# A message-passing kernel on one core: every place in its written-out instruction order chosen anew

## The chip, the cores and the metric

One NeuronCore of a Trainium2 chip (trn2). The metric is device time in microseconds (us) of one launch; lower is better. The five engines that matter here are TensorE (PE; its weight loads are listed as PEld), VectorE (DVE), ScalarE (ACT), GpSimd (POOL) and SyncE (SP, which here only issues DMAs).

## The reference

128 graphs of 64 nodes with 128 features, an adjacency of about one pair in eight. For every pair a three-layer network makes a message from both nodes' features, the messages are masked by the adjacency and summed over the neighbours, and a second network of the same form updates each node.

```python
def _mlp(x, w0, b0, g0, be0, w1, b1, g1, be1, w2, b2):
    h = jax.nn.relu(x @ w0 + b0)
    h = _layernorm(h, g0, be0)
    h = jax.nn.relu(h @ w1 + b1)
    h = _layernorm(h, g1, be1)
    return h @ w2 + b2
...
pair_feats = jnp.concatenate([f_i, f_j], axis=-1)
messages = _mlp(pair_feats, msg_w0, ...)
messages = messages * coupling_matrix[..., None]
agg = jnp.sum(messages, axis=2)
updated = part_feats + _mlp(jnp.concatenate([part_feats, agg], axis=-1), upd_w0, ...)
```

## The kernel before

The kernel computes messages only for the pairs that the adjacency holds. Two graphs make a pair of graphs p (64 of them), four such pairs make a block b (16), and the edges of a graph are packed into 640 places. The places are cut into 160 chunks n of 4 x 128 edges; five chunks make a group q (32 groups), over which the small vectors of the normalization are computed. Ten chunks belong to one block, so the work repeats with a period of ten chunks.

For each block, VectorE numbers the edges along each row of the adjacency (`rank`, line 731, a scan) and forms a flag for weights other than 0 and 1 (`odd_weights`, 811 and 812); a small matmul counts them, and GpSimd turns the counts into places (`place`, 749 to 767, and `place_out`, 776). For each pair of graphs ScalarE and VectorE form a 128 x 640 table of which node owns which place (`distance` 876, then `make_tp` 882). GpSimd widens it (`node_rows`, 891), TensorE and VectorE find the neighbour's number (`marks` 908, `compare` 916), and SP's DMAs lay both halves into the selection matrix s (`stack`, 898). TensorE then gathers the first layer's rows for each chunk (`gather`, 933), ScalarE applies the bias and the relu (`relu0`, 938), TensorE transposes (`turn_h`, 943, into the one bank hT), and VectorE takes the statistics (`stats0`, 629, out st<-hT). ScalarE or GpSimd prepares the second layer's shift (`seed` 980, `seed_all` 973), TensorE multiplies (`layer1`, 986), ScalarE or VectorE applies the relu (`relu1`, 997 or 613), and VectorE takes the statistics again (`stats1`, 629, out st<-y). When the last of a group's ten `stats1` is there, GpSimd adds up the variance (`var1_step`, 646 and 647, tile m_v), ScalarE takes the root (`root1_of`, 653, tile m_sq), VectorE inverts it (`inverse_of`, 658), GpSimd makes the weights (`weights`, 1029), and TensorE sums the messages of a whole block (`reduce_block`, 1044: 96 matmuls on end, once in a period). The node update follows with `bias0` (1082, 1083) and `residual` (1087) on GpSimd, three layers (1111) and `finish` (1159) with the store (1162).

There is no scheduler at run time. Each engine runs its instructions in the order in which they were written, and waits at the first one whose inputs or buffers are not ready. That order is written by a plan. Every step is entered with a chunk number n and a tag; its key is 144 n plus a number from the table `WHEN`, read by the step's name and tag, and in the steady part (chunks 14 to 137) by n modulo 10, otherwise by 100 plus the step's own index. The steps are then sorted by this key and issued.

```python
def at(n, tag, fn, *args):
    ...
    t = WHEN.get(f"{fn.__name__}{tag}", {}).get(n % 10 if 14 <= n < 138 else 100 + v, 0)
    plan.append((SCALE * n + t, len(plan), fn, args))
...
for _, _, fn, args in sorted(plan, key=lambda v: v[:2]):
    fn(*args)
```

The buffers that bear on the order: one bank each for hT, for hps (the gather's result) and for mk (`marks`), two for z, two i tables and two j tables, three u tiles, four selection matrices s.

Of the kernel before, what the change touches and what calls it, by code (L numbers as in the profile page):

```python
# [25 lines left out]
    "<lambda>.3": {100: 398},  # L26
    "<lambda>.4": {100: 795},
    "<lambda>.6": {100: 4632},
    "<lambda>.7": {100: 284},
    "ahead.0": {100: 233},  # L30
    "ahead.1": {100: 132},
    "ahead.10": {100: 11},
    "ahead.11": {100: -1},
    "ahead.2": {100: 50},
    "ahead.5": {100: 113},
    "ahead.8": {100: 157},
    "ahead.9": {100: 215},
    "bias0": {3: -1471, 112: -1906, 113: -1642, 114: -17},
    "bias0_0": {115: 1153},
    "bias0_2": {115: 525},  # L40
    "bounds": {100: -15375},
# [8 lines left out]
    "count": {8: -190, 101: 140, 102: 122, 115: -186},  # L50
    "count.0": {100: 47},
    "count_out": {9: -228, 101: -2, 102: 190, 115: -239},
    "count_out.0": {100: 63},
    "degrees": {9: -358, 101: -137, 102: 105, 115: -608},
    "degrees.0": {100: -699},
    "distance": {0: -539, 3: 150, 5: -495, 8: -349, 103: 84, 104: 283, 105: -140, 106: 202,
        107: -511, 108: 189, 158: -852, 159: -528, 160: -749, 161: -525, 162: -737, 163: -1005},
    "distance.0": {100: 181},
    "distance.1": {101: 189},
    "distance.2": {102: 311},  # L60
    "empties.0": {100: 111},
    "empties.1": {100: 152},
    "empties.10": {100: 200},
    "empties.11": {100: 169},
    "empties.2": {100: -14},
    "empties.3": {100: 100},
    "empties.4": {100: 111},
    "empties.5": {100: 55},
    "empties.6": {100: -50},
    "empties.7": {100: -92},  # L70
    "empties.8": {100: -22},
    "empties.9": {100: 128},
    "finish": {8: 220, 110: 217, 111: 771, 112: 335, 113: -14, 114: 4865},
    "finish_0": {115: 6154},
    "finish_2": {115: 6519},
    "flag_in": {100: 118},
    "flag_max": {100: 160},
    "flag_out": {100: 377},
    "flag_sum": {100: 514},
    "flag_turn": {100: 45},  # L80
# [26 lines left out]
    "inverse_of": {0: -228, 5: 130, 125: -359, 126: -111, 127: 59, 128: 506, 129: 147, 130: 64,  # L107
# [44 lines left out]
    "layer_out.uh": {7: -98, 112: 370, 113: 251, 114: 103},  # L152
    "layer_out.uy": {2: 270, 111: -27, 112: 407, 113: 290, 114: 1108},
# [1505 lines left out]
```

## Time and profile before

| what | value |
|---|---|
| three runs | 501.89, 500.96, 501.84 us; median 501.84 |
| the profiled execution's own time | 501.05 us |
| its span, first to last instruction | 499.3 us |
| granted TensorE clock, mean | 0.997 |
| busy in the span: PE, DVE, ACT, POOL | 97%, 94%, 80%, 70% |
| span less busy time, PE | 13.2 us, of it 3.2 us between 50 us and 475 us |
| span less busy time, DVE | 31.3 us |

The span is the time between the first and the last instruction of the program; 1.75 us of the execution's own time lie around it. An engine's share is the time in which at least one of its instructions was running, so an instruction that runs slowly because something holds it up counts as busy. Matmuls overlap, and their ends are modelled: a stall of TensorE is seen in full only as the distance between two starts, and up to about 0.16 us of it is hidden in the busy time (a 128 x 128 matmul is drawn 275 ns long, and the next starts 112 ns after it).

### The profile page before, as it was taken

The page shows a single profiled execution, that of the slowest core. Times are in us where ns is not written, and L with a number is a line of the kernel's source. Part 1 is how long each engine was busy: PE and PEld are TensorE (multiplying, and loading weights), DVE is VectorE, ACT ScalarE, POOL GpSimd, SP SyncE. Part 2 cuts the span into 40 slices and gives each one's busy share as a digit, 9 for nine tenths or more (in the row PEclk, how much of TensorE's full clock was granted, in tenths as well). Part 3 has the DMA queues.
Part 4 walks back from the last instruction along what each step waited for, and adds up shares of the span by engine and source line. Part 5 has one row for each costly group of instructions (what it writes and reads, how often), then busy time and mean ns, then how long its engine had stood idle before and what let it go on. Part 6 is the DMA issues. An engine that isn't in the chain of part 4 may idle for free.

```text
span 499.3 us, 15949 instructions
## 1 busy us (share of the span) xinstructions
PE 486.1 (97%) x5947; PEld 460.6 (92%) x5947; DVE 468.0 (94%) x1225; ACT 397.1 (80%) x907; POOL 349.1 (70%) x563
## 2 busy tenths in 40 slices
PE   7999999999999999999999999999999999999996
PEld 4889999999999999989999998999989999999995
DVE  7999999999999999999999999999999998989985
ACT  6989978878787887868878786887868779867845
POOL 3275776967949776696877859776696859555771
PEclk9999999999999999999999999999999999999998
DMA  4766838376564756646486673666655458626231
GB/s 122 152 140 152 183 100 162 82 165 153 125 139 98 139 142 150 148 113 142 97 167 142 125 152 90 136 137 147 142 122 135 95 120 163 145 68 154 59 41 47
DMA packets 91474, 63.55 MB, mean 127 GB/s; under 512 B 57473, under 2 KB 75522, under 8 KB 91394
## 3 DMA queue, kind: packets, MB, share of 16 engines
q1 hardware_dynamic: 91106, 62.36, 57.7%
q8 instruction: 49, 0.80, 0.7%
q14 instruction: 31, 0.25, 0.2%
q10 hardware_dynamic: 288, 0.13, 0.1%
HBM read 7.15 MB, written 4.19 MB: 23 GB/s over the span
## 4 chain that ended last, share of the span: by engine, by line


## 5 line engine op out<-in xcount | busy, mean ns | idle before, releaser
L986 PE MATMUL z<-w1c,h 128*128 128x128 f32 x1280 | 190.1, 275 | 0.0
L986 PEld LDWEIGHTS z<-w1c,h 128*128 128x128 f32 x1280 | 172.4, 192 | 4.1 <-DVE uy_st L629 0.2
L938 ACT ACTIVATE h<-hps,b0c 128x512 f32<-128x512 f32 x160 | 108.9, 681 | 35.0 <-PE hps L933 34.5
L629 DVE BATCH_NORM_STATS2 st<-hT 128x6 f32<-128x256 f32 x320 | 122.4, 415 | 6.7 <-PE hT L943 5.1
L629 DVE BATCH_NORM_STATS2 st<-y 128x6 f32<-128x256 f32 x320 | 126.9, 418 | 1.6 <-ACT y L997 1.5
L980 ACT ACTIVATE z<-b1b,m_sd 128x128 f32<-128x128 f32 x320 | 117.3, 368 | 9.4 <-DVE y L613 3.7
L943 PE MATMUL hT<-ident,h 128*128 128x128 f32 x640 | 113.0, 276 | 1.9 <-DVE st L629 1.8
L933 PE MATMUL hps<-s,abl 128*128 128x512 f32 (+3 forms) x256 | 96.9, 381 | 2.6 <-ACT h L938 2.2
L933 PE MATMUL hps<-s,abh 128*128 128x512 f32 (+3 forms) x256 | 89.9, 358 | 0.0
L973 POOL TENSOR_TENSOR u<-b1b,m_sd 128x512 f32<-128x512 f32 x80 | 84.3, 1057 | 7.7 <-ACT m_sd L637 7.7
L943 PEld LDWEIGHTS hT<-ident,h 128*128 128x128 f32 x640 | 75.9, 141 | 6.3 <-issue 3.1
L1029 POOL TENSOR_TENSOR w<-oh,m_q 128x192 f32<-128x192 f16 x126 | 62.0, 513 | 8.8 <-DVE m_q L658 2.5
L916 DVE TENSOR_TENSOR j<-mk,cmpt 128x320 fp32r<-128x320 f32 x124 | 59.2, 477 | 6.3 <-PE mk L908 3.6
L891 POOL CAST i<-tp 128x640 fp32r<-128x640 f16 x58 | 41.7, 719 | 32.1 <-DMA s<-i 30.1
L997 ACT ACTIVATE y<-z 128x512 f32<-128x512 f32 x80 | 47.4, 595 | 17.7 <-PE z L986 17.3
L613 DVE CUSTOM_DVE_ANT_0 y<-z,u 128x512 f32<-128x512 f32 x80 | 54.0, 675 | 3.6 <-PE z L986 3.3
L933 PEld LDWEIGHTS hps<-s,abl 128*128 128x128 f32 x256 | 48.8, 191 | 7.7 <-ACT h L938 3.7
L876 ACT ACTIVATE d<-slot,mid 128x640 f16<-128x640 f16 x64 | 52.1, 818 | 1.7 <-POOL mid L765 1.0
L933 PEld LDWEIGHTS hps<-s,abh 128*128 128x128 f32 x256 | 49.1, 192 | 0.2
L647 POOL TENSOR_TENSOR m_v<-m_v,st 128x20 f32<-128x20 f32 x31 | 7.2, 232 | 58.5 <-DVE st L629 57.3
L1044 PE MATMUL ys<-y,w 128*32 128x128 f32 x1488 | 44.1, 274 | 0.0
L1044 PEld LDWEIGHTS ys<-y,w 128*32 128x32 f32 x1488 | 39.6, 110 | 2.5 <-issue 2.1
(193 smaller groups left out, 890.7 us busy)
## 6 DMA issues: line engine op xcount, KB each, us to landing
s<-i SPq DMA_DIRECT2D x124, 160.0 KB, 3.1
s<-j SPq DMA_DIRECT2D x124, 160.0 KB, 2.9
xn<-in_x_dram SPq DMA_DIRECT2D x15, 256.0 KB, 3.9
out_dram<-uo SPq DMA_DIRECT2D x15, 256.0 KB, 2.5
an<-in_adj_dram SPq DMA_DIRECT2D x16, 128.0 KB, 3.4
oh<-tp SPq DMA_TRANSPOSE x64, 3.2
xn<-in_x_dram SPq DMA_DIRECT2D x2, 128.0 KB, 3.0
out_dram<-uo SPq DMA_DIRECT2D x2, 128.0 KB, 2.0
```

What stands on the lines that cost most here:

```text
L613: nc.vector._custom_dve(TENSOR_ADD_SAT, out=o, in0=ps, in1=sb, s0=BIG, s1=0.0)
L629: nc.vector.bn_stats(st, src.rearrange("p t c -> p c t"))
L876: nc.scalar.activation(D[p], slot, AF.Abs, bias=blocks[b]["mid"][:, q:q + 1], scale=-1.0)
L916: nc.vector.tensor_tensor(JR[p][:, c], MK.pop((p, k))[:, 0:HC], cmpt[:, c], op=ALU.is_equal)
L933: nc.tensor.matmul(HP[n][:, c:c + w], lhsT=blocks[g // (2 * PB)]["ab", g // 4 % 2][k][:, g % 4, :], rhs=S[g // 2][:, g % 2, e:e + w], star ...
L938: nc.scalar.activation(H[n], HP.pop(n), AF.Relu, bias=b0c)
L943: nc.tensor.transpose(HT[n][:, t, :], H[n][:, t * P:(t + 1) * P], ident)
L973: nc.gpsimd.tensor_tensor(U[n], bc(W["b1b"], CH), SR[q][:, k:k + CH].unsqueeze(2).to_broadcast([P, CH, C]), op=ALU.mult)
L980: nc.scalar.activation(z_of(n)[:, t, :], W["b1b"], AF.Copy, scale=SR[q][:, k:k + 1])
L986: nc.tensor.matmul(ps[:, t, :], lhsT=H[n][:, t * P:(t + 1) * P], rhs=W["w1c"], start=by_vector(n) and t == 0, stop=True, skip_group_check= ...
L1029: (nc.vector if p == NP - 2 else nc.gpsimd).tensor_tensor(WT[p][:, g], oh, qs, op=ALU.mult)
L1044: nc.tensor.matmul(YS[b][g * N + m * HN:g * N + (m + 1) * HN, k, :], lhsT=w[:, g, m, u, :], rhs=y, start=(u == 0), stop=(u == TH - 1), til ...
```

## The change

Only the numbers in `WHEN` are replaced: all of its entries are chosen anew, and the table is two lines shorter, so line numbers of the kernel after are smaller by 2 (`stats1` at 629 is at 627). No instruction is added, removed or changed in size; the buffers, the choice of engine for each step and the chunk at which a step is entered stay. By the words that go with the change, VectorE's `rank`, `make_tp` and `odd_weights` are to be kept clear of GpSimd's operations, and later landings of DMAs are allowed for.

```diff
-    "rank": {6: -208, 101: 117, 102: -33},
+    "rank": {6: -172, 101: 62, 102: -12},
...
-    "residual": {9: 658, 111: 1661, 112: 1065, 113: 1049, 114: 3450},
+    "residual": {9: -202, 111: 2069, 112: 835, 113: 1274, 114: 2138},
```

What the numbers do is seen in the order of the engines. **VectorE in a period of the steady part, around `rank`,** from the two `stats0` rows ahead of it to the last `stats1` of the group. In before the group's statistics tile is st_4540, st_4724 is the next group's, st_4583 holds `stats0`, tp is written by `make_tp`, j by `compare`; the scan of `rank` is printed here as SCALAR_TENSOR_TENSOR.

```order
L629 BN_STATS st_4583<-hT 128x6 x2
L731 SCALAR_TENSOR_TENSOR rk<-first,an 128x256
L629 BN_STATS st_4540<-y 128x6
L882 TENSOR_SCALAR tp<-d,deg 128x640
L629 BN_STATS st_4540<-y 128x6
L1359 MEMSET ones_row 1x128
L629 BN_STATS st_4540<-y 128x6
L629 BN_STATS st_4724<-y 128x6
L629 BN_STATS st_4583<-hT 128x6
L629 BN_STATS st_4540<-y 128x6
L629 BN_STATS uy_st<-uy 128x6
L629 BN_STATS st_4583<-hT 128x6
```

The same place after, where st_4527 is this group's tile, st_4575 holds `stats0` and st_4725 is the next group's:

```order
L627 BN_STATS uy_st<-uy 128x6
L627 BN_STATS st_4575<-hT 128x6 x2
L627 BN_STATS st_4527<-y 128x6
L914 TENSOR_TENSOR j_4750<-mk,cmpt 128x320
L627 BN_STATS st_4527<-y 128x6
L729 SCALAR_TENSOR_TENSOR rk<-first,an 128x256
L627 BN_STATS st_4575<-hT 128x6 x2
L914 TENSOR_TENSOR j_4750<-mk,cmpt 128x320
L880 TENSOR_SCALAR tp<-d,deg 128x640
L627 BN_STATS st_4527<-y 128x6
```

Five statistics that followed `rank` now stand ahead of it: three of the group's, one of the next group's, one of the node update's. The two `stats0` of the next chunk follow it at once. Of the two `compare` of a pair, the first stood ahead of the five statistics that preceded `rank` and now has one of them behind it; the second stood behind the group's last `stats1` and now precedes it, as `make_tp` and `rank` did already. (The MEMSET fills a row of constants and bears on nothing here.)

**GpSimd at the same place,** from `node_rows` (i) to the variance of the group (m_v). In before:

```order
L891 CAST i_4594<-tp 128x640
L973 TENSOR_TENSOR u<-b1b,m_sd 128x512
L1082 TENSOR_TENSOR m_4604<-c2u,deg 128x512
L1083 TENSOR_TENSOR m_4604<-m_4604,ub0r 128x512
L1087 TENSOR_TENSOR xo<-xn,cu2b 128x512
L973 TENSOR_TENSOR u<-b1b,m_sd 128x512
L776 TENSOR_TENSOR posall<-pos,an 64x4x64 x2
L646 TENSOR_SCALAR m_v<-st_4019 128x20
L647 TENSOR_TENSOR m_v<-m_v,st_4540 128x20
```

and after:

```order
L971 TENSOR_TENSOR u<-b1b,m_sd 128x512 x2
L1027 TENSOR_TENSOR w<-oh,m_q 128x192
L774 TENSOR_TENSOR posall<-pos,an 64x4x64 x2
L889 CAST i_4727<-tp 128x640
L1080 TENSOR_TENSOR m_4732<-c2u,deg 128x512
L1081 TENSOR_TENSOR m_4732<-m_4732,ub0r 128x512
L971 TENSOR_TENSOR u<-b1b,m_sd 128x512
L644 TENSOR_SCALAR m_v<-st_4011 128x20
L645 TENSOR_TENSOR m_v<-m_v,st_4527 128x20
```

Between `node_rows` and the variance stand three operations where seven stood: `residual` (xo) has gone, the two `seed_all` (u) and the two `place_out` (posall) are ahead of `node_rows`, and one later `seed_all` has come in.

**GpSimd half a period later,** ahead of the second variance of the period, from the low half of the first layer's rows (abl). In before:

```order
L864 TENSOR_TENSOR abl<-ab,abh 128x512
L973 TENSOR_TENSOR u<-b1b,m_sd 128x512
L646 TENSOR_SCALAR m_v<-st_4322 128x20
L647 TENSOR_TENSOR m_v<-m_v,st_4724 128x20
L891 CAST i_5025<-tp 128x640
```

and after:

```order
L862 TENSOR_TENSOR abl<-ab,abh 128x512
L971 TENSOR_TENSOR u<-b1b,m_sd 128x512
L1085 TENSOR_TENSOR xo<-xn,cu2b 128x512
L1027 TENSOR_TENSOR w<-oh,m_q 128x192 x2
L644 TENSOR_SCALAR m_v<-st_4331 128x20
L645 TENSOR_TENSOR m_v<-m_v,st_4725 128x20
```

Here `residual` and two `weights` have come in between.

TensorE's order changes in small ways throughout: in the steady part, pairs of transposes of the node update trade places with half a `layer1`, or a `gather` with a transpose. On SP the load of the next adjacency is issued a few DMAs earlier, and two transposing DMAs of `node_marks` stand together ahead of the two halves of a j table (`stack`) that one of them parted. At the end, all four matmuls of the second-last block's third layer stand ahead of the last chunk's `layer1`, where two stood in the middle of it and two behind, and on VectorE that block's `finish` stands ahead of five of the last `stats1` instead of two. At the start, ScalarE's copy of the turned features comes ahead of the first two `distance`, and the third `distance` ahead of the first `node_rows`-like copy (line 1347).

More of the change, by code (lines that the diff above doesn't have):

```diff
@@ L25 @@
 WHEN = {
[L26 to L41, printed above, removed]
[8 rows of a table removed]
@@ L50 @@
[L50 to L75, printed above, removed]
@@ L370 @@
-    "weights.1.1": {2: -269, 7: -112, 151: -490, 153: 294, 155: 117, 157: 234, 159: 279, 161: 259,
-        163: 359},
+    "<lambda>.3": {100: -2537},
+    "<lambda>.4": {100: 3097},
+    "<lambda>.6": {100: 5123},
+    "<lambda>.7": {100: -79},
+    "ahead.0": {100: 256},
+    "ahead.1": {100: 84},
+    "ahead.10": {100: 0},
+    "ahead.11": {100: 76},
+    "ahead.2": {100: 60},
+    "ahead.5": {100: -84},
+    "ahead.8": {100: 146},
+    "ahead.9": {100: 84},
+    "bias0": {3: -1230, 112: -1975, 113: -1986, 114: 89},
@@ new lines @@
+    "bias0_0": {115: 1022},
+    "bias0_2": {115: 1262},
+    "bounds": {100: -14609},
[8 rows of a table added]
+    "count": {8: -202, 101: 130, 102: 110, 115: -196},
+    "count.0": {100: 66},
+    "count_out": {9: -224, 101: 56, 102: 96, 115: -273},
+    "count_out.0": {100: 79},
+    "degrees": {9: -369, 101: -144, 102: -4, 115: -419},
+    "degrees.0": {100: 58},
+    "distance": {0: -532, 3: 185, 5: -470, 8: -359, 103: 34, 104: 302, 105: -163, 106: 312,
+        107: -610, 108: 189, 158: -893, 159: -639, 160: -591, 161: -589, 162: 13, 163: -1137},
@@ new lines @@
+    "distance.0": {100: 163},
+    "distance.1": {101: 208},
+    "distance.2": {102: 283},
+    "empties.0": {100: 156},
+    "empties.1": {100: 154},
+    "empties.10": {100: -158},
+    "empties.11": {100: 84},
+    "empties.2": {100: 96},
+    "empties.3": {100: 133},
+    "empties.4": {100: 79},
+    "empties.5": {100: 37},
+    "empties.6": {100: 17},
+    "empties.7": {100: 5},
+    "empties.8": {100: -10},
+    "empties.9": {100: 125},
+    "finish": {8: 213, 110: 222, 111: 777, 112: 384, 113: -54, 114: 3979},
@@ new lines @@
+    "make_tp": {1: -260, 4: 205, 6: -429, 9: -243, 103: 96, 104: 208, 105: -87, 106: 173, 107: -43,
[10 rows of a table added]
+    "node_marks": {0: -442, 4: -407, 5: 312, 9: 798, 100: -754, 101: 181, 152: -18, 153: 713,
+        154: -781, 155: 359, 156: 606, 157: 277, 158: -117, 159: 340, 160: 797, 161: 698,
+        162: -325, 163: -35},
+    "node_rows": {0: -296, 2: 343, 5: 133, 7: -72, 102: 288, 103: 288, 104: 78, 105: 39, 106: 84,
+        107: -121, 158: -211, 159: -393, 160: -396, 161: -330, 162: 551, 163: -4},
@@ new lines @@
+    "odd_weights": {3: -40, 101: -1472, 102: -1343, 115: -641},
+    "odd_weights.0": {100: -1313},
+    "ones": {100: 12204},
+    "place": {1: -108, 101: 70, 102: 9, 115: -476},
+    "place_first": {100: 131},
+    "place_out": {3: 192, 101: -54, 102: 171, 115: -267},
+    "place_pair.0": {100: 156},
+    "place_rest": {100: 194},
+    "rank": {6: -172, 101: 62, 102: -12},
+    "rank.0": {100: -1715},
+    "reduce.-1": {163: 258},
+    "reduce.-2": {162: 253},
+    "reduce.-3": {161: 347},
+    "reduce.-4": {160: 292},
@@ new lines @@
+    "rows.0": {101: -218},
+    "rows.0.0.0.2": {100: 285},
+    "rows.0.0.2.4": {100: 359},
+    "rows.1": {100: -12, 101: -134},
+    "rows_both": {8: -539, 114: -514, 115: -584},
[24 rows of a table added]
+    "seed_all": {1: 170, 3: 350, 4: -162, 6: 138, 8: -68, 100: 112, 101: 310, 103: 133, 106: 604,
[34 rows of a table added]
+    "sums_out": {4: 97, 112: -659, 113: -39, 114: -235},
[39 rows of a table added]
+    "turn_out.uh": {1: -406, 111: -195, 112: 338, 113: 375, 114: 390},
+    "turn_out.uy": {6: 50, 111: -504, 112: 264, 113: 168, 114: 1560},
+    "turn_out.ysum": {5: 127, 112: -511, 113: -93, 114: -20},
@@ new lines @@
+    "turn_out_0.uh": {115: 1461},
+    "turn_out_0.uy": {115: 3868},
+    "turn_out_0.ysum": {115: 254},
+    "turn_out_2.uh": {115: 2199},
+    "turn_out_2.uy": {115: 6095},
+    "turn_out_2.ysum": {115: 974},
+    "turn_x": {6: -532, 101: -146, 115: -480},
+    "turn_x.0": {100: 217},
+    "turn_x.0.0.2": {100: 134},
+    "turn_x_out": {7: -568, 101: -247, 115: -579},
+    "turn_x_out.0.0.2": {100: 157},
+    "turn_x_out_rest": {100: 99},
+    "upd_inverse": {4: 483, 111: 1277, 112: 884, 113: 356, 114: 3830},
@@ new lines @@
+    "upd_inverse_0": {115: 5531},
+    "upd_inverse_2": {115: 6376},
+    "upd_m1": {2: 560, 111: 1362, 112: 992, 113: 501, 114: 2165},
+    "upd_m1_0": {115: 3031},
+    "upd_m1_2": {115: 5644},
+    "upd_root0": {9: 115, 111: -54, 112: 669, 113: 332, 114: 319},
+    "upd_root0_0": {115: 1662},
+    "upd_root0_2": {115: 2433},
+    "upd_root1": {4: 336, 111: 1229, 112: 727, 113: 84, 114: 3171},
+    "upd_root1_0": {115: 5123},
+    "upd_root1_2": {115: 6137},
+    "upd_shift": {9: 201, 111: 202, 112: 691},
@@ new lines @@
+    "upd_shift.0": {113: 649, 114: 467},
+    "upd_shift.2": {113: 664, 114: 486},
+    "upd_shift_0.0": {115: 1697},
+    "upd_shift_2.0": {115: 3776},
+    "var1_step": {3: 385, 8: -21, 100: 379, 125: -63, 126: 15, 127: 331, 128: 639, 129: 332,
+        130: 295, 131: 299},
+    "weights.0.0": {0: -182, 5: 383, 150: -302, 152: 484, 154: 380, 156: 586, 158: 495, 160: 390,
+        162: 206},
+    "weights.0.1": {1: -242, 6: 256, 150: -383, 152: 756, 154: 125, 156: 610, 158: 268, 160: 360,
+        162: 235},
@@ L372 @@
+    "weights.1.0": {1: 157, 6: 107, 151: -408, 153: 813, 155: 45, 157: 397, 159: 286, 161: 342,
+        163: 246},
+    "weights.1.1": {2: 216, 7: -41, 151: -453, 153: 426, 155: 55, 157: 410, 159: 185, 161: 610,
+        163: 239},
 }
```

110 lines of the change are left out of this document (23 added, 87 removed), and 420 rows, old and new, of the table WHEN.

## The prediction

> **What bounds the kernel now.** I read the page's busy shares first, then TensorE's steps in order of time, then the waits, and last the stretches ahead of a stall on each engine.
>
> ```profile
> span 499.3 us, 15949 instructions
> PE 486.1 (97%) x5947; PEld 460.6 (92%) x5947; DVE 468.0 (94%) x1225; ACT 397.1 (80%) x907; POOL 349.1 (70%) x563
> ```
>
> TensorE is the bound and VectorE is close behind it. A new order removes no work, so all it can win is time in which TensorE stands still; that time is found between equal places of the periods. The timeline of TensorE has the sums of a block (96 matmuls, once in a period) at these places, first, two in the middle, last:
>
> ```profile
> 120.27 2.83 PE L1044 MATMUL ys<-y,w 128*32 128x128 f32 x96
> ...
> 150.25 2.83 PE L1044 MATMUL ys<-y,w 128*32 128x128 f32 x96
> 179.56 2.83 PE L1044 MATMUL ys<-y,w 128*32 128x128 f32 x96
> ...
> 389.43 2.83 PE L1044 MATMUL ys<-y,w 128*32 128x128 f32 x96
> ```
>
> Nine periods lie between the first and the last row: 269.16 us, 29.91 us each. The one from 150.25 to 179.56 took 29.31 us with the same instructions in the same order. I take 29.31 us as what TensorE needs without a stall. Nine periods hold 269.16 - 9 x 29.31 = 5.4 us of stalls.
>
> The table of waits names who is late:
>
> ```profile
> ACT m_sq L653 <- POOL m_v L647: 11.6, 12, 1.7
> PE hps L933 <- ACT h L938: 2.2, 5, 0.7
> PE hT L943 <- DVE st L629: 1.8, 4, 0.7
> ```
>
> Once a period ScalarE stands at the root (m_sq) for GpSimd's variance; TensorE waits for VectorE's statistics to free hT, or for a `relu0` that is queued behind that root. The period from 208.98 us shows how it comes to the hT wait: VectorE, GpSimd, ScalarE and TensorE in order of time.
>
> ```profile
> 212.22 1.68 DVE L731 TENSOR_TENSOR_SCAN rk<-first,an 128x256 f16<-128x256 f32 x1
> 213.83 0.41 DVE L629 BATCH_NORM_STATS2 st<-y 128x6 f32<-128x256 f32 x1
> 214.15 1.02 DVE L882 TENSOR_SCALAR tp<-d,deg 128x640 f16<-128x640 f16 x1
> ...
> 217.10 0.41 DVE L629 BATCH_NORM_STATS2 st<-hT 128x6 f32<-128x256 f32 x1
> ```
> ```profile
> 209.27 0.72 POOL L891 CAST i<-tp 128x640 fp32r<-128x640 f16 x1 [3.59 <-DMA s<-i]
> ...
> 210.95 1.04 POOL L1082 TENSOR_TENSOR m<-c2u,deg 128x512 f32<-128x512 f32 x1
> 212.07 1.28 POOL L1083 TENSOR_TENSOR m<-m,ub0r 128x512 f32<-128x512 f32 x1
> 213.32 1.68 POOL L1087 TENSOR_TENSOR xo<-xn,cu2b 128x512 f32<-128x512 f32 x1
> ...
> 216.04 1.52 POOL L776 TENSOR_TENSOR posall<-pos,an 64x256 f16<-64x256 f32 x2
> ...
> 218.00 0.23 POOL L647 TENSOR_TENSOR m_v<-m_v,st 128x20 f32<-128x20 f32 x1
> ```
> ```profile
> 216.22 0.69 ACT L938 ACTIVATE h<-hps,b0c 128x512 f32<-128x512 f32 x1
> 218.26 0.31 ACT L653 ACTIVATE m_sq<-m_v,eps_c 128x20 f32<-128x20 f32 x1 [1.35 <-POOL m_v L647]
> ```
> ```profile
> 216.47 0.60 PE L1094 MATMUL ma<-ident,ysum 128*128 128x128 f32 x4
> 217.66 0.63 PE L943 MATMUL hT<-ident,h 128*128 128x128 f32 x4 [0.59 <-DVE st L629]
> ```
>
> `rank` and `make_tp` take 1.68 and 1.02 us while GpSimd adds 512-wide tiles, and the last `stats0` ends only at 217.51. ScalarE idles from 216.91 to 218.26, because GpSimd reaches the variance only after `residual`, a `seed_all` and two `place_out`.
>
> How long VectorE's two steps take when alone is their minimum (view of a line: minimum, median, maximum in ns); the groups give the means:
>
> ```profile
> L731 DVE TENSOR_TENSOR_SCAN rk<-first,an x16: 671/974/1739, 3.6 to 392.9; 128x256 f16<-128x256 f32 x16
> L882 DVE TENSOR_SCALAR tp<-d,deg x64: 355/514/1100, 6.9 to 439.3; 128x640 f16<-128x640 f16 x64
> ...
> L882 DVE TENSOR_SCALAR tp<-d,deg 128x640 f16<-128x640 f16 x64 | 38.1, 595 | 0.6 <-ACT d L876 0.4
> L731 DVE TENSOR_TENSOR_SCAN rk<-first,an 128x256 f16<-128x256 f32 x16 | 16.5, 1033 | 1.7 <-DMA an<-in_adj_dram 1.7
> ```
>
> So held-up time is 64 x (0.595 - 0.355) = 15.4 us for `make_tp` and 16 x (1.033 - 0.671) = 5.8 us for `rank`. Most of these 21 us lie beside TensorE's own work. They count only by the stalls above, so I do not add them to the sum.
>
> It is not always VectorE that is held:
>
> ```profile
> 271.72 0.68 DVE L731 TENSOR_TENSOR_SCAN rk<-first,an 128x256 f16<-128x256 f32 x1
> 271.73 1.76 POOL L1083 TENSOR_TENSOR m<-m,ub0r 128x512 f32<-128x512 f32 x1
> ```
>
> Here `rank` began first and took 0.68 us, and GpSimd's addition was stretched to 1.76 us. The Trainium skill (SBUF — State Buffer, section "Who interferes with whom") says that VectorE and GpSimd share a pair of ports, that whichever starts first keeps it for its whole instruction, and that the other stands still. The two stretches agree, one each way. By that rule a step of VectorE that is moved ahead of GpSimd's may only hand the wait over to GpSimd; what that would cost here is the second rival.
>
> **The change part by part.** *VectorE and GpSimd around `rank`, steady part.* In the new order GpSimd has between `node_rows` and the variance three wide operations. At 0.72 us for `node_rows` (209.27's row) and 1.04 us for a wide one that is not held (210.95's row) it would be at the variance by 209.27 + 0.72 + 3 x 1.04 = 213.1 us, an estimate on the old time scale, where the second `place_out` now ends at 217.56 us. On VectorE five statistics stand ahead of `rank` that followed it; at 0.34 us from start to start (213.83 to 214.15 is 0.32) that is 1.7 us, and one wait of 0.40 us for a landing ahead of an earlier `compare` can go. `rank` would begin near 212.22 + 1.7 - 0.4 = 213.5 us, 0.4 us after GpSimd has come to rest. `make_tp` would follow near 215.3 us (0.67 for `rank`, 0.7 for two `stats0`, 0.43 for a `compare`), while GpSimd waits for the `stats1` behind it. Both would run alone. The group's last `stats1` then ends near 216.1 us and the variance near 216.4 us, ahead of ScalarE's `relu0` end at 216.91: the root no longer waits. The last `stats0` ends near 215.1 us, against TensorE's need at about 217.1 us (216.47 + 0.60): that stall goes with 2 us to spare. What is late next is TensorE itself.
>
> So the 5.4 us may go whole. At the other end nothing goes, or new stalls of the same size come. I take 4.9 us, near the full end, since the period from 150.25 us shows that TensorE has nothing else to wait for; bounds 5.4 and 0.
>
> *`compare` put off.* Its bank must be free at the next `marks`:
>
> ```profile
> 239.97 0.47 DVE L916 TENSOR_TENSOR j<-mk,cmpt 128x320 fp32r<-128x320 f32 x1
> ...
> 245.23 0.30 PE L908 MATMUL mk<-tp,posall 128*128 128x320 f16 x1
> ```
>
> 4.8 us lie between, and the step is put off by some nine statistics, 3 us. Hidden, at nothing; with VectorE 2 us late it would be TensorE's wait.
>
> *`residual` and two `weights` ahead of the second variance.* The idle time there covers them:
>
> ```profile
> 226.26 0.26 POOL L646 TENSOR_SCALAR m_v<-st 128x20 f32<-128x20 f32 x1
> 229.79 0.23 POOL L647 TENSOR_TENSOR m_v<-m_v,st 128x20 f32<-128x20 f32 x1 [3.28 <-DVE st L629]
> ...
> L1029 POOL TENSOR_TENSOR w<-oh,m_q 128x192 f32<-128x192 f16 x126 | 62.0, 513 | 8.8 <-DVE m_q L658 2.5 <-issue 2.4 <-PE z L986 2.2
> ```
>
> `residual`, 1.68 us in the held row at 213.32 and at the least as long as the other addition at 212.07, 1.28 us, and two `weights` at 0.51 us are 2.3 to 2.7 us in 3.28 us: nothing, with 0.6 to 1.0 us left. Behind the variance ScalarE's root is queued, and behind that `relu0`.
>
> *TensorE's own order and SP's.* The same matmuls in nearly the same runs (1980 rows of equal neighbours before, 2006 after). Every switch could cost or save up to a tenth of a microsecond; 26 more of them bound this at 2.6 us either way, and I take zero, since both orders mix the same kinds. The DMAs moved on SP are the same in number; the j halves that no longer have a transposing DMA between them land earlier, and TensorE has almost no wait for a landing in the steady part to win.
>
> *Start and end.* TensorE's busy time in the first two stretches of 25 us, and a wait in the second:
>
> ```profile
> 0.00:25.00 25.00, 20.91 (x199) 16.32 (x200) 20.87 (x58) 20.82 (x44) 7.57 (x22) 1.00 0.64 137
> 25.00:50.00 25.00, 23.93 (x264) 21.86 (x262) 23.40 (x59) 23.39 (x55) 16.61 (x26) 1.00 0.64 146
> ...
> PE ma L819 <- DMA xn<-in_x_dram: 0.4, 1, 0.4
> ```
>
> Of 5.2 us idle here, 4.1 us are in the first stretch, mostly the first chain from the loads, which the order does not shorten. The x load behind the wait is now issued ahead of two other DMAs. I take 0.5 us won, half of the second stretch's 1.07 us; bounds 2.0 won, and 1.5 lost, since ScalarE's third `distance` now stands ahead of a copy and the first `relu0` can come later. At the end:
>
> ```profile
> 479.69 0.61 PE L986 MATMUL z<-w1c,h 128*128 128x128 f32 x4
> 480.13 0.38 PE L1094 MATMUL ma<-ident,ysum 128*128 128x128 f32 x2
> 480.35 0.61 PE L1111 MATMUL mu<-u2c,uyT 128*128 128x128 f32 x4
> ```
>
> Two matmuls (480.35 to 480.80) and two transposes (480.13 to 480.35) come ahead of the last `layer1`, which ends 0.67 us later; from it hang the last statistics, the root and the last weights. VectorE was busy with `finish` until 482.1 us there, and `finish` now comes earlier, so most of it is covered: 0.3 us lost, bounds 0 and 0.7.
>
> The sum against the profiled execution: 501.05 - 4.9 - 0.5 + 0.3 = 495.95 us. Its time lies 0.79 us under the median of the three runs, 501.84, so the forecast for the median is 496.7 us.
>
> **The rivals.** *No change.* The order does what it says on VectorE, but GpSimd comes to rest too late: `node_rows` waits up to 3.6 us for a landing (209.27's row), and only 0.4 us part `rank` from GpSimd. If those landings come later, `rank` is held as before, and the periods stall as before. For it: the narrow gap. Against: the group's variance is then still reached earlier by GpSimd, and hT has 2 us. Time: 501.84 less or plus the start and end, 501.6 us. Chance 0.10.
>
> *Slower: the second variance takes the place of the first.* GpSimd's queue ahead of it has grown by 2.3 to 2.7 us in an idle time of 3.28 us. VectorE's `make_tp` and `stats1` come earlier here by the time no longer lost, which shrinks that idle time by about 1 us; by the rule above VectorE may also start first and hold GpSimd here. Then the root and the `relu0` behind it are late in each of some 13 periods. It decides from 0.4 us a period on, where 13 x 0.4 = 5.2 us eats the gain; at 0.8 us a period it is 501.84 - 5.1 + 10.4 = 507 us. For it: little cover is left. Against: two `weights` that stood earlier in the same stretch have left it, which gives 1 us back. Chance 0.10.
>
> *Slower by TensorE's switches alone* (2.6 us) does not reach the other side unless the stalls stay; that joint case I leave at 0.02, at 504 us.
>
> **How the numbers follow.** The forecast has 0.78. Its own range: all of the 5.4 us and 2.0 us at the start won, 494.4, and a little from the stalls after 390 us, 494.0; at the other end half of the steady gain, 1.5 us lost at the start and 0.3 us at the end, 500.9. To the no-change case it needs 501.6. About 0.88 lies in it by these chances, and I keep some doubt about unseen stalls. Faster by over 0.2% (1.0 us, about what a measurement of this kernel tells from no change): 0.78. Within 0.2%: 0.09, the no-change case with a little left out. Slower: 0.13.
>
> **What would show it.** Right: blocks' sums 29.3 to 29.5 us apart; the wait of ScalarE's m_sq for m_v down from 11.6 us to under 4 us; `rank` near a mean of 0.7 us and `make_tp` under 0.5 us; PE's busy share up to 98%. Wrong in the first step: `rank` still over 1 us on average, with GpSimd's wide operations beside it. Wrong in the second: m_sq waits of the same sum, now ahead of the second root. Wrong in TensorE's order: periods over 29.6 us without waits in the table. A time over 501 us would refute the forecast.

## The result, and the profile after

| | before | after |
|---|---|---|
| median of 6 runs, one beside the other | 501.40 us | 496.17 us |
| lowest and highest | 498.78, 504.58 | 495.49, 496.87 |
| ratio, with its 95% interval | | 0.990 (0.988 to 0.992) |
| the profiled execution, its span | 501.05, 499.3 | 496.87, 495.0 |

The forecast was 496.7 us. From the page of the kernel after, the span and the first of the busy shares:

```profile
span 495.0 us, 15915 instructions
PE 484.8 (98%) x5947; PEld 461.3 (93%) x5947; DVE 462.3 (93%) x1225; ACT 397.9 (80%) x907; POOL 353.0 (71%) x563
```

TensorE has 10.2 us of span without work, where it had 13.2. Where they went is seen between the sums of a block, from TensorE's timeline (start, duration, line): the first and the last of the nine periods.

```profile
120.11 2.83 PE L1042 MATMUL ys<-y,w 128*32 128x128 f32 x96
...
384.09 2.83 PE L1042 MATMUL ys<-y,w 128*32 128x128 f32 x96
```

Nine periods take 263.98 us, 29.33 us each, and the longest is 29.40; before they took 269.16 us. That is 5.18 us won in the steady part. The table of waits (total, times, longest):

```profile
DVE st L627 <- PE hT L941: 12.7, 22, 1.2
...
ACT m_sq L651 <- POOL m_v L645: 2.1, 11, 0.5
```

ScalarE's wait at the root fell from 11.6 to 2.1 us, and the hT wait has turned round: VectorE now waits for TensorE, 12.7 us in all, where it waited 5.1 us before. The groups of VectorE that share the time with GpSimd's wide operations (busy time, mean in ns), after and then before:

```profile
L880 DVE TENSOR_SCALAR tp<-d,deg 128x640 f16<-128x640 f16 x64 | 29.7, 465 | 0.1
L809 DVE SCALAR_TENSOR_TENSOR a<-an 128x256 f32<-128x256 f32 x16 | 12.7, 795 | 0.0
L729 DVE TENSOR_TENSOR_SCAN rk<-first,an 128x256 f16<-128x256 f32 x16 | 11.9, 742 | 1.5 <-DMA an<-in_adj_dram 1.5
```
```profile
L811 DVE SCALAR_TENSOR_TENSOR a<-an 128x256 f32<-128x256 f32 x16 | 7.2, 451 | 0.0
```

On average `rank` and `make_tp` come near their times alone, but `odd_weights` (a), which the words of the change name with them, takes longer than before. The period from 208.08 us on VectorE, GpSimd, ScalarE and TensorE shows the rest:

```profile
212.32 0.67 DVE L729 TENSOR_TENSOR_SCAN rk<-first,an 128x256 f16<-128x256 f32 x1
213.86 0.76 DVE L627 BATCH_NORM_STATS2 st<-hT 128x6 f32<-128x256 f32 x2 [0.87 <-PE hT L941]
...
214.93 0.38 DVE L880 TENSOR_SCALAR tp<-d,deg 128x640 f16<-128x640 f16 x1
```
```profile
212.36 1.46 POOL L971 TENSOR_TENSOR u<-b1b,m_sd 128x512 f32<-128x512 f32 x1
...
215.79 0.23 POOL L645 TENSOR_TENSOR m_v<-m_v,st 128x20 f32<-128x20 f32 x1 [1.60 <-DVE st L627]
```
```profile
215.57 0.69 ACT L936 ACTIVATE h<-hps,b0c 128x512 f32<-128x512 f32 x1 [0.45 <-PE hps L931]
216.16 0.30 ACT L651 ACTIVATE m_sq<-m_v,eps_c 128x20 f32<-128x20 f32 x1
```
```profile
215.81 0.60 PE L941 MATMUL hT<-ident,h 128*128 128x128 f32 x4
```

The last statistics of hT end at 214.62 us, 1.2 us ahead of the transposes that need the bank. GpSimd stands at the variance and waits 1.60 us for VectorE, so `make_tp` runs alone there, and the root starts at once behind `relu0`. `rank` is not clear of GpSimd: it began 0.04 us ahead of a `seed_all` (u), and that took 1.46 us, not 1.04. The Trainium skill (SBUF — State Buffer, section "Who interferes with whom") says that issue order decides which of the two engines blocks, and the row agrees. One period does not: in the one from 237.41 us `seed_all` is recorded 0.04 us ahead of `rank` (at 241.68 and 241.73 us) and is still the one that is held, for 1.54 us. A lead of 0.04 us is too short to test the rule in this profile.

At the two ends: up to 120.11 us 0.16 us are won, and from the last of the nine periods to VectorE's last instruction 105.93 us pass, where 106.40 us did: 0.47 us won. These are the last rows of VectorE's timeline, before and then after:

```profile
495.22 0.61 DVE L1159 SCALAR_TENSOR_TENSOR uo<-z,um_q,xo 128x128 f32<-128x128 f32 x2
```
```profile
489.41 0.61 DVE L1157 SCALAR_TENSOR_TENSOR uo<-z,um_q,xo 128x128 f32<-128x128 f32 x2
```

The work ends 5.81 us earlier, and 1.5 us of it are given back by stores that land later: by the view of the DMAs the last two stores took 2.0 us to land before and 3.9 us after (median of the two), and 3.47 us lie between VectorE's end and the end of the span before, 4.98 us after. So the profiled executions differ by 5.18 + 0.16 + 0.47 - 1.51 = 4.3 us in span. In the twelve runs below these two stores took 2.9 to 4.1 us, whatever the order; it was the profile of before that had a short one.

### The profile page after: what moved, and what is told of

The parts are those of the page before. It is cut to its first block, busy times and chain, and to the rows that moved or that the text cites. A ratio compares the mean times of both kernels' runs of the same rounds, so it can differ in the third digit from the quotient of the medians.

```text
span 495.0 us, 15915 instructions
## 1 busy us (share of the span) xinstructions
PE 484.8 (98%) x5947; PEld 461.3 (93%) x5947; DVE 462.3 (93%) x1225; ACT 397.9 (80%) x907; POOL 353.0 (71%) x563
## 4 chain that ended last, share of the span: by engine, by line
## 5 line engine op out<-in xcount | busy, mean ns | idle before, releaser
L627 DVE BATCH_NORM_STATS2 st<-hT 128x6 f32<-128x256 f32 x320 | 122.2, 418 | 15.3 <-PE hT L941 12.7
L627 DVE BATCH_NORM_STATS2 st<-y 128x6 f32<-128x256 f32 x320 | 125.3, 419 | 0.0
L971 POOL TENSOR_TENSOR u<-b1b,m_sd 128x512 f32<-128x512 f32 x80 | 87.5, 1103 | 7.8 <-ACT m_sd L635 7.7
L931 PE MATMUL hps<-s,abh 128*128 128x512 f32 (+3 forms) x256 | 92.2, 365 | 0.0
L941 PEld LDWEIGHTS hT<-ident,h 128*128 128x128 f32 x640 | 77.2, 141 | 2.9 <-PE z L984 0.6
L1027 POOL TENSOR_TENSOR w<-oh,m_q 128x192 f32<-128x192 f16 x126 | 65.2, 533 | 17.2 <-DVE m_q L656 9.6
```

The source lines that it names most:

```text
L627: nc.vector.bn_stats(st, src.rearrange("p t c -> p c t"))
L931: nc.tensor.matmul(HP[n][:, c:c + w], lhsT=blocks[g // (2 * PB)]["ab", g // 4 % 2][k][:, g % 4, :], rhs=S[g // 2][:, g % 2, e:e + w], star ...
L941: nc.tensor.transpose(HT[n][:, t, :], H[n][:, t * P:(t + 1) * P], ident)
L971: nc.gpsimd.tensor_tensor(U[n], bc(W["b1b"], CH), SR[q][:, k:k + CH].unsqueeze(2).to_broadcast([P, CH, C]), op=ALU.mult)
L1027: (nc.vector if p == NP - 2 else nc.gpsimd).tensor_tensor(WT[p][:, g], oh, qs, op=ALU.mult)
```

## The experiments

Two stalls had been read from before: TensorE waits for the hT bank (VectorE late), and ScalarE's root waits for GpSimd, with `relu0` and so the `gather` behind it. The first experiments give single engines the other kernel's order. For that the loop takes the steps from a list; the steps of the engine named stand in it in the order of one kernel, those of the other engines in the order of the other kernel, and across engines a step stands behind those whose data or buffers it needs:

```diff
-        for _, _, fn, args in sorted(plan, key=lambda v: v[:2]):
-            fn(*args)
+        for i in ORDER:
+            plan[i][2](*plan[i][3])
```

"Nine periods" is the time between the sums of a block that start near 120 and 385 us (269.16 us before, 263.98 us after), each time of one profiled execution; ratios are to before, beside it.

**1. VectorE's order alone.**

> The kernel before, with VectorE's instructions alone in the order of the kernel after; GpSimd, ScalarE, TensorE and the DMAs keep the order of before. Theory (the stalls have two sources, VectorE held beside GpSimd and GpSimd late at the variance, and each order heals part): GpSimd still comes to the variance behind residual, a seed_all and two place_out, so ScalarE's m_sq wait stays near 11 us; rank stands later but still beside residual, so its mean stays near 1 us; only the hT wait goes. It wins 2.5 us (1 to 4) of the 5.2 us. Rival (VectorE's order does it all): 5 us, rank near 0.7 us. Rival (GpSimd's late variance does it all): 0 us.

Measured: 504.02 us, ratio 1.005 (1.003 to 1.007). The nine periods, from TensorE's timeline; then one period's root on ScalarE and its `gather` on TensorE:

```profile
121.20 2.83 PE L1044 MATMUL ys<-y,w 128*32 128x128 f32 x96
...
390.31 2.83 PE L1044 MATMUL ys<-y,w 128*32 128x128 f32 x96
```
```profile
220.16 0.31 ACT L653 ACTIVATE m_sq<-m_v,eps_c 128x20 f32<-128x20 f32 x1 [1.37 <-POOL m_v L647]
```
```profile
222.07 0.44 PE L933 MATMUL hps<-s,abl 128*128 128x384 f32 x1 [0.45 <-ACT h L938]
```

269.11 us: nothing won, and the total is 2.7 us longer, 0.9 us of it ahead of the nine periods and 1.7 us behind them. VectorE is in time now at the hT bank (it waits 13.2 us in all for TensorE, 5.1 us before), the root's waits (10.2 us) and the mean of `rank` (1.00 us) are as expected, and yet the 2.5 us did not come. Where they went is seen when TensorE's starts are compared, one by one, with those of the undisturbed period from 150.25 us of before; TensorE's order is the same in all of these runs. The sums over the nine periods, in us:

| | hT bank, 7 to 10 us into a period | `gather` behind the root, near 10.5 us | a transpose near 24.6 us |
|---|---|---|---|
| before | 2.8 | 2.5 | 0.0 |
| VectorE's order alone | 0.6 | 3.2 | 1.6 |
| GpSimd's order alone (second) | 2.6 | 0.1 | 0.0 |
| both orders (third) | -0.1 | 0.1 | 1.6 |

So the hT stall went nearly as forecast, by 2.2 us. Of these, 0.7 us came out again at the `gather`: in before a period showed mostly the one stall or the other, and now six periods of nine have the second. The larger part, 1.6 us, is a new short wait in every period, of which the forecast had nothing. A transpose follows the `gather` ahead of it by 0.40 us where in before it does by 0.26 us; the third experiment shows the cause:

```profile
205.69 0.42 PE L933 MATMUL hps<-s,abl 128*128 128x384 f32 x1
206.09 0.30 PE L943 MATMUL hT<-ident,h 128*128 128x128 f32 x1
```

**2. GpSimd's order alone.**

> The kernel before, with GpSimd's instructions alone in the order of the kernel after. Theory: the variance waits for VectorE's last stats1 and no longer for GpSimd's own queue, so the m_sq wait falls below 5 us; make_tp comes after GpSimd has come to rest and runs near its 0.36 us, but rank at its old place still meets the wide additions (mean near 1 us). It wins 4 us (2.5 to 5.2). Rival (GpSimd's late variance does it all): 5 us. Rival (VectorE's order does it all): 0 us, hT waits as before.

Measured: 500.72 us, ratio 0.999 (0.997 to 1.001). Nine periods, then the hT stall on VectorE and on TensorE:

```profile
119.99 2.83 PE L1044 MATMUL ys<-y,w 128*32 128x128 f32 x96
...
386.59 2.83 PE L1044 MATMUL ys<-y,w 128*32 128x128 f32 x96
```
```profile
182.52 1.06 DVE L731 TENSOR_TENSOR_SCAN rk<-first,an 128x256 f16<-128x256 f32 x1
...
183.82 0.77 DVE L882 TENSOR_SCALAR tp<-d,deg 128x640 f16<-128x640 f16 x1
...
186.51 0.41 DVE L629 BATCH_NORM_STATS2 st<-hT 128x6 f32<-128x256 f32 x1
```
```profile
187.07 0.63 PE L943 MATMUL hT<-ident,h 128*128 128x128 f32 x4 [0.22 <-DVE st L629]
```

266.60 us: 2.56 us won in the steady part, the root hardly waits any more (1.5 us in all), and the hT stall stays, 2.6 us by the table above. That is less than the 4 us expected: `make_tp` at its old place does not run alone, as the expectation had it, but takes 0.77 us in most periods. The total stands still because the end, with its mixed orders, takes 108.7 us in place of 106.4.

**3. Both orders.**

> The kernel before, with VectorE's and GpSimd's instructions in the order of the kernel after; ScalarE, TensorE and the DMAs keep the order of before. Theory: these two orders are the change; periods of 29.3 to 29.4 us, 5.2 us won (4.4 to 5.8), m_sq wait below 4 us. Rival (TensorE's or ScalarE's own order carries a part): at most 3.5 us won, periods over 29.5 us.

Measured: 502.13 us, ratio 1.001 (1.000 to 1.003). Nine periods, and one place on VectorE and TensorE; behind them the same place in before:

```profile
121.32 2.83 PE L1044 MATMUL ys<-y,w 128*32 128x128 f32 x96
...
386.42 2.83 PE L1044 MATMUL ys<-y,w 128*32 128x128 f32 x96
```
```profile
203.69 0.42 DVE L629 BATCH_NORM_STATS2 st<-y 128x6 f32<-128x256 f32 x1
204.03 0.74 DVE L629 BATCH_NORM_STATS2 st<-hT 128x6 f32<-128x256 f32 x2
```
```profile
204.51 0.42 PE L933 MATMUL hps<-s,abl 128*128 128x384 f32 x1
204.92 0.30 PE L943 MATMUL hT<-ident,h 128*128 128x128 f32 x1
```
```profile
203.92 0.42 PE L933 MATMUL hps<-s,abl 128*128 128x384 f32 x1
204.18 0.27 PE L943 MATMUL hT<-ident,h 128*128 128x128 f32 x1
```

265.10 us, every period 29.45: 4.1 us won, and one new wait, by which a period is some 0.13 us longer. VectorE's new order has a statistics of y ahead of the two of hT; they end at 204.77, and the transpose follows at 204.92, 0.41 us behind the `gather` ahead of it, where in before it is 0.26 us. The runs in which VectorE keeps its order, or moves one step alone (second and eleventh), don't have this wait. (The table of waits doesn't name it; a wait this short shows only as a distance between starts.) The forecast of 5.2 us failed by that and by the ends: 1.0 us lost at the start and 3.1 us at the end, where this kernel's orders belong to two plans.

**4. After, with TensorE's order of before.**

> The kernel after, with TensorE's instructions put back into the order of before; all else as after. Theory (TensorE's order is worth nothing): within 0.7 us of the kernel after, 496.2 us, periods 29.3 to 29.4 us. Rival (fewer switches between kinds of matmul carry part of the gain): 1 to 2.6 us slower than after, 497.2 to 498.8 us, with periods over 29.45 us and no waits in the table to explain it.

Measured: 500.06 us, ratio 0.997 (0.996 to 0.999). Nine periods:

```profile
120.02 2.83 PE L1042 MATMUL ys<-y,w 128*32 128x128 f32 x96
...
385.12 2.83 PE L1042 MATMUL ys<-y,w 128*32 128x128 f32 x96
```

3.9 us slower than after: my term of zero did not come out, and the loss is larger than the rival's 1 to 2.6 us. 265.10 us again: 1.1 us of it is the same wait of 0.13 us a period; 2.9 us are lost at the end. Switches between kinds of matmul are not it: before had periods of 29.31 us with this very order. And `rank` is held here, 1.06 us on average, and the periods are no longer than in the third run, where it took 0.78 us.

**5 and 6. The steady part alone,** by the same loop, with start and end from before: first VectorE's and GpSimd's order, then TensorE's with them.

> The kernel before, with VectorE's and GpSimd's instructions in the order of the kernel after for the steps of the steady part alone (chunks 14 to 137); start and end keep the order of before. The third experiment's periods were 29.45 us, 4.1 us won over nine, and its total stood still because the end took 3.1 us and the start 1.0 us longer. Theory (the loss came from mixed orders at start and end): 4.1 us won, 497.3 us (496.5 to 498.3), periods 29.45 us, 106.4 us from the last of the nine to VectorE's end as in before. Rival (the steady part itself hands the lost time to the end, through work put off): total within 1.5 us of before, 109 us at the end.

> As the fifth, with TensorE's steady order of after as well; ScalarE and the DMAs keep the order of before. Theory (TensorE's order matters only because it fits VectorE's: the 0.13 us wait for hT in each period goes): periods 29.32 us, 496.2 us (495.4 to 497.2). Rival (the 0.13 us comes from ScalarE's order or from the DMAs): periods 29.45 us, 497.3 us.

Measured: 499.19 us, ratio 0.996 (0.994 to 0.997), and 498.17 us, 0.993 (0.991 to 0.995). Nine periods and the next sum of a block, of the fifth and then of the sixth:

```profile
120.22 2.83 PE L1044 MATMUL ys<-y,w 128*32 128x128 f32 x96
...
385.28 2.83 PE L1044 MATMUL ys<-y,w 128*32 128x128 f32 x96
...
411.48 2.83 PE L1044 MATMUL ys<-y,w 128*32 128x128 f32 x96
```
```profile
120.01 2.83 PE L1044 MATMUL ys<-y,w 128*32 128x128 f32 x96
...
384.11 2.83 PE L1044 MATMUL ys<-y,w 128*32 128x128 f32 x96
...
410.65 2.83 PE L1044 MATMUL ys<-y,w 128*32 128x128 f32 x96
```

265.06 and 264.10 us: the two engines win 4.1 us, and TensorE's order takes out the 0.13 us a period, 29.31 in eight of the nine. The theory of the sixth holds for the periods. Both totals miss the forecast by 2 us, mostly for the end: the step out of the steady part takes 26.2 and 26.5 us, where it took 24.87 in before and 24.58 in after. The rival of the fifth is half right: from the last of the nine periods to VectorE's end 107.7 us pass, where the theory had 106.4 and the rival 109. The old numbers of the end don't fit the new steady part; after, with new numbers throughout, does not have this loss.

**7. After, with `rank` alone back at its old number.**

```diff
-    "rank": {6: -172, 101: 62, 102: -12},
+    "rank": {6: -208, 101: 62, 102: -12},
```

> The kernel after, with rank alone back at its old number in the steady part: ahead of one stats1, one compare and one more stats1, at 211.25 us on the scale of after's trace, beside GpSimd's second bias addition (211.11 to 212.40). Theory (a held step of VectorE costs nothing as long as the next statistics are in time: VectorE waits 0.87 us for hT behind rank): rank's mean 1.3 us or more, periods stay 29.3 us, total within 0.7 us of after, 496.2 us. Rival (a held rank is what stalls TensorE): 0.4 to 0.6 us a period, 3.6 to 5.4 us slower than after.

Measured: 496.68 us, ratio 0.990 (0.988 to 0.993), and nine periods in 264.02 us. One period of VectorE:

```profile
211.63 1.36 DVE L729 TENSOR_TENSOR_SCAN rk<-first,an 128x256 f16<-128x256 f32 x1
...
213.91 0.76 DVE L627 BATCH_NORM_STATS2 st<-hT 128x6 f32<-128x256 f32 x2 [0.19 <-PE hT L941]
```

`rank` takes twice as long as it needs (1.36 us; the mean over all sixteen is 1.15 us, under the 1.3 us expected), and the periods show no cost: the wait for hT behind it shrinks from 0.87 to 0.19 us. The theory of cover holds, the rival falls.

**8. After, with `residual` alone back at its old number.**

```diff
-    "residual": {9: -202, 111: 2069, 112: 835, 113: 1274, 114: 2138},
+    "residual": {9: 658, 111: 2069, 112: 835, 113: 1274, 114: 2138},
```

> The kernel after, with residual alone back at its old number in the steady part: 1.27 us more GpSimd work ahead of the period's first variance, and less ahead of the second. Theory (GpSimd has 1.60 us of idle time there, waiting for VectorE's last stats1): it fits, m_sq waits stay below 3 us in all, total within 0.7 us of after, 496.2 us. Rival (residual ahead of the variance is what made ScalarE's root late): m_sq waits back at 8 us or more, 2.5 us slower than after.

Measured: 496.86 us, ratio 0.990 (0.988 to 0.993), m_sq waits 2.4 us, nine periods in 264.18 us. VectorE's group of `rank`:

```profile
L729 DVE TENSOR_TENSOR_SCAN rk<-first,an 128x256 f16<-128x256 f32 x16 | 18.5, 1155 | 1.6 <-DMA an<-in_adj_dram 1.6
```

`rank` now runs beside the second addition of `bias0`, which comes later by the time of `residual`, and is held; `make_tp` takes 0.55 us on average, 0.47 in after. The total is 0.7 us longer, at the edge of what was expected and within the spread of the runs, and the nine periods 0.2 us. Of the seven operations that stood ahead of the variance, `residual` alone was not the one that had to go: the idle time covers one more.

**9 and 10. How late GpSimd may be.** One and three additions that nothing reads, ahead of each variance of the groups 3 to 26 (k is 1, then 3):

```diff
+        spare = const.tile([P, CH, C], F16, name="spare")
+
         def var1_step(q):
+            for _ in range(k if 3 <= q <= 26 else 0):
+                nc.gpsimd.tensor_tensor(spare, bc(W["b1b"], CH), bc(W["b1b"], CH), op=ALU.add)
```

> The kernel after, with one more 512-wide addition on GpSimd, some 1.1 us, right ahead of each variance of the groups 3 to 26. It writes a tile that nothing reads; the output is unchanged. Theory (a late variance is covered by GpSimd's idle time ahead of the last stats1, 1.60 us at the first variance of a period and 2.19 us at the second): hidden, total within 0.8 us of after, 496.2 us, m_sq waits below 4 us. Rival (the place of GpSimd's work has no cover left, the second rival of the prediction): 0.4 to 0.8 us a period, 5 to 10 us slower.

> The kernel after, with three such additions, some 3.3 us, ahead of each of these variances; the output is unchanged. Theory: the variance is 1.7 us late at the first place and 1.1 us at the second, m_sq waits over 10 us in all, relu0 is queued behind the root and TensorE stalls at the gather as in before, 0.5 to 1.5 us a period: 6 to 18 us slower than after, 502 to 514 us. Rival (a late root doesn't reach TensorE, and the gain came from elsewhere): within 2 us of after.

Measured: 496.44 us, ratio 0.991 (0.989 to 0.994), and 511.82 us, ratio 1.023 (1.020 to 1.025). The additions of the ninth, from the groups of GpSimd, and the waits of the tenth:

```profile
L1007 POOL TENSOR_TENSOR spare<-b1b 128x512 f16<-128x512 f32 x24 | 25.0, 1042 | 0.0
```
```profile
ACT m_sq L651 <- POOL m_v L645: 27.4, 24, 2.2
...
PE hps L931 <- ACT h L936: 7.3, 13, 1.4
```

25 us more on GpSimd are hidden whole. With 3.1 us a variance the root waits 24 times, `relu0` behind it, and TensorE at the `gather`; the nine periods take 275.96 us, 12.0 us more than after. That is the mechanism of the second rival of the prediction, with its price, here at both variances of a period; the point from which it decides lies between 1.0 and 3.1 us of more work ahead of a variance.

**11. Before, with GpSimd's steady order and one `make_tp`.** The loop of the first experiments; of VectorE's steps only the `make_tp` entered at chunks 14, 24, 34 and so on is moved, behind seven statistics.

> The kernel before, with GpSimd's steady order of after, and of VectorE's steps one alone moved: the make_tp that stands ahead of the second pair of stats0 behind rank goes behind them, its place in after (rank, compare and all statistics keep the order of before). Theory (the hT wait that GpSimd's order alone leaves is the held make_tp and rank standing ahead of that stats0; taking out the one of 0.5 to 1.0 us is enough): periods 29.3 to 29.4 us, 497.6 us (496.8 to 498.6) with the 1.3 to 1.6 us that the old end costs behind the new steady part. Rival (it takes the rest of VectorE's order): periods 29.6 us on average as in the second experiment, 500 us.

Measured: 497.25 us, ratio 0.993 (0.991 to 0.996). Nine periods:

```profile
120.01 2.83 PE L1044 MATMUL ys<-y,w 128*32 128x128 f32 x96
...
383.77 2.83 PE L1044 MATMUL ys<-y,w 128*32 128x128 f32 x96
```
```profile
211.23 1.06 DVE L731 TENSOR_TENSOR_SCAN rk<-first,an 128x256 f16<-128x256 f32 x1
...
215.01 0.38 DVE L882 TENSOR_SCALAR tp<-d,deg 128x640 f16<-128x640 f16 x1
```

263.76 us, 29.28 us in most periods: the whole 5.4 us of stalls, with `rank` still held (0.97 us on average) and TensorE, ScalarE and the DMAs in the order of before. The theory holds; the rest of VectorE's order isn't needed for it. At its new place `make_tp` is also no longer held (the second row), so this run alone doesn't tell whether its place or its length stalled TensorE. With the end of after it might be as fast as after or a little faster; that wasn't tried.

**12. After, with `rank` and that `make_tp` back.**

```diff
-    "make_tp": {1: -260, 4: 205, 6: -429, 9: -243, 103: 96, 104: 208, 105: -87, 106: 173, 107: -43,
+    "make_tp": {1: -260, 4: 131, 6: -429, 9: -243, 103: 96, 104: 208, 105: -87, 106: 173, 107: -43,
...
-    "rank": {6: -172, 101: 62, 102: -12},
+    "rank": {6: -208, 101: 62, 102: -12},
```

> The kernel after, with rank and the make_tp behind it both back at their old numbers in the steady part (rank ahead of a compare and two stats1, make_tp ahead of the two stats0 and a compare). Both then run beside GpSimd's wide additions. Theory (VectorE has 0.87 us of waiting for hT and 1.2 us more until TensorE needs the bank, against 0.7 us for rank and 0.4 to 1.0 us for make_tp): no stall or one of at most 0.1 us a period, within 1 us of after, 496.2 us; rank's mean over 1.1 us and make_tp's over 0.5 us. Rival (held steps ahead of stats0 stall TensorE whatever the rest): 0.4 to 0.8 us a period, 3.6 to 7 us slower than after.

Measured: 497.27 us, ratio 0.993 (0.990 to 0.995); nine periods in 264.36 us, one of them 29.62. The two steps in one period:

```profile
211.99 1.37 DVE L729 TENSOR_TENSOR_SCAN rk<-first,an 128x256 f16<-128x256 f32 x1
...
214.00 0.37 DVE L880 TENSOR_SCALAR tp<-d,deg 128x640 f16<-128x640 f16 x1
```

`rank` is held (1.15 us on average), `make_tp` is not (0.47 us), against the expectation, so it tests less than it was meant to: a held `rank` and an early `make_tp` that runs alone. No period stalls at the hT bank behind them. The nine periods are 0.4 us longer than after, 0.3 us of it in the one period, which stalls elsewhere, as one period of the sixth did; the total is 1.1 us above after, just over the 1 us expected.

## Why the prediction was right, and where its reasons were not

**What bounds the kernel.** Right. The nine periods fell to 29.33 us, against 29.31 read from the one undisturbed period of before, and 5.18 of the 5.4 us came, where I took 4.9.

**The two stalls.** Right in kind, and the two make up the 5.4 us: before has 2.8 us at the hT bank and 2.5 us at the `gather`. The first and second experiments each remove one of them, and the tenth brings the one at the root back by delaying the variance. They cover one another a little, 0.7 us in the first experiment. What I hadn't seen is the new wait that VectorE's order puts in, 1.6 us over nine periods, and that TensorE's new order takes out again.

**"Both would run alone."** Right for `make_tp`, wrong for `rank`. Behind the two `stats0`, `make_tp` takes 0.37 to 0.38 us in all nine periods, with GpSimd standing at the variance as forecast. `rank` is not clear of GpSimd. Counted from the sum of the block it begins at 4.24 us, where the working has 4.5 (213.5 less 208.98). But GpSimd comes to rest only at 5.74 us, where the working has 4.1 (213.1 less 208.98): `node_rows` starts 0.94 us later in its period than before, behind the operations moved ahead of it, and two of the three wide ones take 1.29 and 1.46 us where I took 1.04. So GpSimd is too late for `rank`, which is what the no-change rival asks for (if not by late landings), and yet the stall did not come. That `rank` is near 0.7 us on average is in part luck: in eight of nine periods it is GpSimd that is held, with the two starts 0.04 us apart. In the period from 149.44 us `rank` takes 1.43 us, and the period is no longer; where it is held in most periods (4, 7, 8, 11, 12) no stall like that of before follows.

What counts is `make_tp`. In the second experiment it is held and stands ahead of the `stats0`, and TensorE stalls; in the eleventh it is moved behind them and runs alone, and the stall is gone; in the twelfth it stands ahead but runs alone, and no stall comes either. These runs fit a stall that needs a `make_tp` both held and in front; the twelfth differs from the second in the rest of VectorE's order too. A held one in front with everything else as after was not measured, so its place and its length are not told apart any further. `odd_weights`, which the words of the change name too, takes 0.80 us on average now, and the periods show no stall from it.

**`compare` put off, at nothing.** Right: no wait of TensorE for that bank appears.

**`residual` and two `weights` ahead of the second variance, at nothing.** Right, and with more room than the 0.6 to 1.0 us I had left: at the second variance GpSimd still waits 1.8 to 2.2 us for VectorE's statistics in each of the nine periods, and one more addition ahead of each variance fits (ninth).

**TensorE's order, at zero.** The total was right and the term wrong. It takes out 1.0 us over the nine periods (fifth against sixth), but only because VectorE's other moves had put that wait in; the eleventh, without those moves, doesn't need it. I had costed it by switches; what it is worth is its fit with VectorE's order.

**Start and end.** The start won 0.16 us of the 0.5 I took, within its bounds. The end lost nothing: VectorE finished 0.47 us sooner, where I had 0.3 us lost; together the two ends came out 0.4 us better than the sum had them. The 1.5 us that the profiled span gives back at its end come from the last stores' landing, which no part of the sum had. And the numbers for the end are worth more than this comparison shows: with before's, the new steady part loses 1.0 to 1.6 us on its way out (fifth, sixth, eleventh).

**The rivals.** No change and the slower ones didn't come, though what the first asks for did. The second is real as a mechanism (tenth), only far off.

## What to carry to other kernels

Find the place in the bounding engine's timeline where an equal period is longer, and ask which instruction stands ahead of the late one in its queue. Here GpSimd's new steady order and one VectorE step of 0.4 to 1.0 us, moved behind the statistics that TensorE waits for, won in the steady part all that the whole new order wins. Judge a cure by the place of its stall and not by the total: VectorE's order alone cured its stall and lost the time again, less at the stall next to it than at a new short wait elsewhere. Orders of several engines belong together: half of a new plan can cost more at its seams than it wins.

## What the runs showed of the hardware that was not expected

- `odd_weights`, with one tile in SBUF read twice, takes 0.40 us at the least and up to 1.20 us in after: 0.45 us on average in before, 0.80 us in after, with 5.5 us more busy time and no cost seen in the periods. That GpSimd's operations beside it hold it, as they do `rank`, fits this but was not tested by itself.
- Sixteen `rank` were busy up to 18.5 us (eighth) against 11.9 us, with the total within 0.7 us: VectorE's busy share says little of what such holding costs.
- The same two stores at the end took 2.0 to 4.1 us to land; about 1.5 us of the difference between two profiled spans goes with this.
